# Numerators one slot behind their logits, a reordered start and a bunched end in a lookup convolution kernel

## The chip, the cores and the metric

One core of a Trainium2 chip runs the whole program. The metric is the device time of one execution in microseconds (us). Each kernel was executed several times, and medians are quoted.

## The reference, cut to what matters

Sixteen images of 256 channels and 28x28 pixels are normalised by groups of eight channels, and go through two "lookup" convolutions and a gate. Each convolution treats every channel by itself: the nine pixels of a 3x3 patch are compared with 16 learned codes, a softmax over the codes gives weights, and the weighted codes are multiplied by a matrix.

```python
def amm_conv3x3(x, centroids, w_sub, stride=1):
    ...                                            # p: patches (B, pixels, C, 9)
    d = jnp.sum(p * p, axis=-1)[..., None] - 2.0 * jnp.einsum('bncs,cks->bnck', p, centroids) \
        + jnp.sum(centroids * centroids, axis=-1)[None, None]
    attn = jax.nn.softmax(-d, axis=-1)
    lut = jnp.einsum('cks,cso->cko', centroids, w_sub)
    out = jnp.einsum('bnck,cko->bno', attn, lut)
    ...
# per image: v = gn(x); y = relu(bn1(conv1(v))); y = bn2(conv2(y))
#            y = y * sigmoid(relu(mean(y) @ w1 + b1) @ w2 + b2); out = x + relu(y + v)
```

## The kernel before

The work is laid out in slots. One slot handles 16 rows of channel pairs for half of an image's pixels: "logits" (TensorE), exponentials (ScalarE), "numerators" (TensorE, which also gives the sum of the exponentials), transposes and a reciprocal (VectorE), scaling (GpSimd), one more transpose, and some slots later the "looks", the large matmuls that accumulate the output. Sixteen slots make a stage, which is one layer of one image. There are 32 stages, and the layers of successive images alternate.

```python
ring = [p_ring.tile([P, 2, 512], F32, name=f"pair{i}") for i in range(3)]   # three pairs of PSUM banks
# pair() hands them out in turn; the two accumulators take the other two banks

epool = ctx.enter_context(tc.tile_pool(name="epool", bufs=2))               # exponentials
xpool = ctx.enter_context(tc.tile_pool(name="xpool", bufs=2))               # images
hpool = ctx.enter_context(tc.tile_pool(name="hpool", bufs=1))               # y, one buffer

def b_logits(u):          # 2 pairs x 16 matmuls 32x32
    u["lg"] = logits(u, MROW + NCH if u["maxed"] else ONE + 1)
def b_exp(u):             # one exponential for each pair
    for ps in u.pop("lg"):
        e = epool.tile([P, 2, 400], F32, tag="e", name="e")
        nc.scalar.activation(e[:, :, :n], ps[:, :, :n], AF.Exp, scale=2.0)
        u["e"].append(e)
def b_num(u):             # 2 pairs x 16 matmuls 32x32
    u["nm"] = [pair(), pair()]
    ...
```

The schedule is a table of jobs by slot and by position within the slot. On each engine the jobs are issued in that order.

```python
LC = 3                                             # looks start three slots behind
LOGITS, LOAD, MOVE, EXP, LOOK_A, NUM, TURN, SMALL, LOOK_B, MAX, LOOK_C, TURN_BACK, REST = range(13)

# stage(): one slot s
at(s, LOGITS, b_logits, u)
at(s, EXP, b_exp, u)
at(s, NUM, b_num, u)
at(s, TURN, b_turn, u)                             # VectorE: transposes of the numerators, reciprocal
at(s, TURN, c_scale, u)
at(s + 1, TURN_BACK, c_turn, u)

def norm(self, b, t):                              # statistics of image b, from slot t on
    self.at(t, REST, gn_stats, b, 0)               # VectorE, first half of the channels
    self.at(t + 1, REST, gn_stats, b, 1)           # VectorE, second half
    self.at(t + 2, SMALL, gn_mean, b)              # TensorE, then ScalarE and GpSimd
    self.at(t + 3, SMALL, gn_var, b)               # TensorE: waits for GpSimd's gn_dv
    self.at(t + 4, REST, gn_apply, b, 0)           # ScalarE writes the normalised image
    self.at(t + 5, REST, gn_apply, b, 1)

n0 = -3 if b == 1 else t - 2 * NS - 3              # the image is loaded two slots ahead
plan.at(n0 - 2, REST, load_x, b, x[b])
plan.norm(b, n0)
plan.prep(0, pat_of(0, b), {1: 1, 2: 32, 3: 56}.get(b, t - 2 * NS + 3))   # patches, written to DRAM
...
for i in range(9 * C // PART):                     # layer-2 weights: load, sort by channel, store
    plan.at(3 + i, REST, load_part, wsub2, i)
    plan.at(4 + i, REST, sort_ws2, i)
moves = ...                                        # 74 transfers that place layer 2's tables
for i, (f, *a) in enumerate(moves):
    plan.at(6 + i // 3, REST, f, *a)               # three in a slot, on the sync queue
```

Patches make a trip: GpSimd writes them to DRAM (`pat`), and the sync queue loads them for each slot (`pt`).

Of the kernel before, what the change touches and what calls it, by code (L numbers as in the profile page):

```python
# [15 lines left out]
P = 128  # L16
# [7 lines left out]
NQ = NT // 4  # L24
NLT = NQ * 9 // 4
# [44 lines left out]
def kernel(  # L70
# [82 lines left out]
    pts = [const.tile([P, 4, 400], F32, name=f"pt{i}") for i in range(6)]  # L153
    for t in pts:
        nc.sync.dma_start(t[ONE::32], view(consts, 0, [[0, 4], [0, 4], [1, 400]]))


# [6 lines left out]
    nhalf_sb = load(nhalf, "nhalf_sb")  # L164
    mones_sb = const.tile([P, 2, 32], F32, name="mones_sb")
    nc.sync.dma_start(mones_sb, mones.rearrange("l p m -> p l m"))
# [10 lines left out]
    perm = sort_sb[:, n_in : n_in + NB * C].rearrange("p (b c) -> p b c", b=NB)  # L177
    wd = [load(wd1, "wd0"), const.tile([P, NT, 32], F32, name="wd1")]
    cw = [load(cw1, "cw0"), load(cw2, "cw1")]
# [62 lines left out]
    def sort_channels():  # L242
# [19 lines left out]
        row = tpool.tile([P, 832], F32, tag="z", name="row")[:, :C]  # L262
        nc.vector.tensor_copy(row, ps[:, :C])
        own = small.tile([P, NB], F32, name="key_own")
# [29 lines left out]
    PART = 384  # L294

# [7 lines left out]
    def sort_ws1(i):  # L303

        t = parts.pop(i)
        for j in range(PART // P):
            ps = bank()
            for b in range(NB):
                nc.tensor.matmul(  # L309
                    ps[:, :C], lhsT=t[:, b, j * P : (j + 1) * P], rhs=perm[:, b], start=(b == 0), stop=(b == NB - 1)  # L310
                )
            w = ws[0][:, i * PART // P + j]
            if j == 1:
                nc.vector.tensor_copy(w, ps[:, :C])
            else:
                nc.scalar.copy(w, ps[:, :C])
# [11 lines left out]
    def sort_c2():  # L328
# [3 lines left out]
        for i in range(2):  # L332
# [7 lines left out]
            nc.scalar.dma_start(view(d_c2[i], 0, [[K * 9, P], [P * K * 9, NB], [1, K * 9]]), t)  # L340

    def sort_ws2(i):
        t = parts.pop(i)
        ps = pair()
        by_position(ps, t, PART)
        r = tpool.tile([P, 832], F32, tag="z", name="part")[:, : NB * PART].rearrange("p (b m) -> p b m", b=NB)
        nc.scalar.copy(r, ps[:, :, :PART])
        nc.scalar.dma_start(view(d_ws2, i * PART, [[9 * C, P], [P * 9 * C, NB], [1, PART]]), r)
# [53 lines left out]
    epool = ctx.enter_context(tc.tile_pool(name="epool", bufs=2))  # L402
# [59 lines left out]
    STEPS = [(dx, k, h) for dx in (1, 0, 2) for k in range(NB) for h in range(2)]  # L462

    def to_pat(l, i, pat, px=0, n=HW):
# [3 lines left out]
        nc.gpsimd.dma_start(  # L468
# [62 lines left out]
    def residual(b, k, i):  # L531
        y = ys[b][0][half(k, i)]
        nc.gpsimd.tensor_add(y, y, xs[b][half(k, i)])

# [188 lines left out]
    LC = 3  # L723
# [4 lines left out]
    class Plan:  # L728
        def __init__(self, step, lead, lb):
# [4 lines left out]
            self.end = self.ns + LC * step  # L734
# [7 lines left out]
        def emit(self):  # L742
# [7 lines left out]
            for n0, of in self.tiles:  # L750

                slots = [n0 + (LC + q) * self.step for q in range(NQ)]
# [11 lines left out]
        def stage(self, l, b, pat, s0, maxed):  # L764
            at = self.at
            for pi, px in enumerate(PXT):
                n0 = s0 + pi * NQ * self.step
                of = []
                for m in range(NQ):
# [17 lines left out]
                    at(s, NUM, b_num, u)  # L787
                    at(s, TURN, b_turn, u)
                    at(s, TURN, c_scale, u)
                    at(s + 1, TURN_BACK, c_turn, u)  # L790
                self.tiles.append((n0, of))

        def prep(self, l, pat, t):

            for i, dx in enumerate((0, 2)):
                for k in range(NB):
                    self.at(t + 4 * i + 2 + k, REST, shift, l, dx, k)
            for i in range(len(STEPS)):
                self.at(t + i, REST, to_pat, l, i, pat)

        def prep_near(self, l, pat, t, slots, t2, slots2):
# [4 lines left out]
            for i in range(len(STEPS)):  # L806
                self.at(t + i * slots // len(STEPS), REST, to_pat, l, i, pat, *PXT[0])
                self.at(t2 + i * slots2 // len(STEPS), REST, to_pat, l, i, pat, *PXT[1])

# [8 lines left out]
        def close(self, b, ob, te, pace):  # L818
# [3 lines left out]
            for n, (k, i) in enumerate((k, i) for k in range(NB) for i in range(2)):  # L822
                self.at(te + 2 + n // 2, REST, gate, b, k, i)
                self.at(te + 3 + n // pace, REST, finish, b, k, i)
                self.at(te + 4 + n // pace, REST, relu, b, k, i)
                self.at(te + 5 + n // pace, REST, residual, b, k, i)
# [11 lines left out]

    for k in range(NB):
        gn_stats(0, k)  # L840
    gn_mean(0)
    gn_var(0)
    for k in range(NB):
        gn_apply(0, k)
    for i, (dx, k, h) in enumerate(STEPS):
        if dx != 1 and h == 0:
            shift(0, dx, k)
        to_pat(0, i, d_pat[0], *PXT[0])
    square_codes(0)
    setup_codes(0)  # L850
    bn_setup()
    sort_channels()
# [3 lines left out]
    for si, (l, b) in enumerate(stages):  # L856
        t = si * NS
        plan.stage(l, b, pat_of(l, b), t, () if l == 0 else MAXED)
        if l == 0 and b >= 1:
            n0 = -3 if b == 1 else t - 2 * NS - 3  # L860
            plan.at(n0 - 2, REST, load_x, b, x[b])
            plan.norm(b, n0)
            plan.prep(0, pat_of(0, b), {1: 1, 2: 32, 3: 56}.get(b, t - 2 * NS + 3))
        if l == 1:
            if b in (0, B - 1):
                t0 = t - NS + LC
                plan.prep_near(1, pat_of(1, b), t0, 4, t0 + 4, 8)
            else:
                plan.prep(1, pat_of(1, b), 44 if b == 1 else t - 2 * NS + LC + 1)
            plan.at(t + NS, REST, load_x, b, x[b])  # L870
            plan.close(b, out[b], t + NS + LC, 1 if b < B - 2 else 2)
    for i in range(len(STEPS)):
        plan.at(i // 3, REST, to_pat, 0, i, d_pat[0], *PXT[1])
    n1 = NLT * P // PART
    for i in range(n1):
        if i < 2:
            plan.at(-6, REST, load_part, ws1, i)
            plan.at(-1, REST, sort_ws1, i)
        else:
            plan.at((i - 2) * 3 // 4 - 1, REST, load_part, ws1, i)  # L880
            plan.at((i - 2) * 3 // 4, (LOOK_A, LOOK_B)[i % 2], sort_ws1, i)
# [115 lines left out]
```

## Time and profile before

| | before |
|---|---|
| median of 3 runs | 2970.67 us (2970.14 to 2972.58) |
| span of the profiled run, granted clock | 2969.2 us, 0.989 |
| first logits start | 57.0 us |
| slots 0 to 16, 16 to 32 | 117.0 us, 103.6 us |
| a later stage, either layer | 88.3 us |
| sum of the 512 numerator groups, each from its start to the next matmul | 555.4 us |

Slot times are taken from the starts of the numerator groups in the trace.

These are groups of instructions by line. After the first bar stand their busy time in us and the mean of one in ns, after the second the engine's idle time just before them and what ended most of it. Kernel before:

```profile
L631 PE MATMUL pair<-e,cw 32*32 32x384 f32 (+1 forms) x16384 | 580.3, 502 | 11.9 <-ACT e L621 10.6
L563 PE MATMUL pair<-pt,wd 19*32 19x384 f32 (+2 forms) x18432 | 561.0, 500 | 5.9 <-DMA pt<-pat 3.3
```

There are 16384 numerator matmuls and 18432 logit matmuls over the same numbers of columns, and the fewer ones have more busy time. That is the wait hidden within "busy". The idle columns show almost nothing.

The table of waits gives total us, times and the longest. Kernel before:

```profile
DVE gn_st L417 <- DMA xt<-in_x: 23.0, 14, 2.5
...
PE pair L434 <- POOL gn_dv L428: 4.2, 14, 0.8
...
PE pair L563 <- DMA pt<-pat: 3.3, 7, 0.7
...
PE pair L563 <- DVE nt L643: 1.6, 5, 0.5
```

VectorE waits 14 times (once for each of 14 images) for an image that has not landed, 23 us in all.

### The profile page before, as it was taken

Reading aid. Unit: us, or ns where it says so; the run is one execution under the profiler, and the core shown is the slowest. Engines: PE = TensorE matmul, PEld = TensorE weight load, DVE = VectorE, ACT = ScalarE, POOL = GpSimd, SP = SyncE. Lnnn points to the kernel's source line nnn. Section 1 sums busy time; section 2 is a strip of 40 time slices with the busy share of each in tenths; the row PEclk is TensorE's granted clock in tenths of the full one; section 3 lists DMA queues with packets and bytes.
Section 4 is the critical chain, followed back from the end, with each engine's and each line's share of the span. In section 5 each row is a group of like instructions: output and inputs, shape, how many; then the busy total and the mean of one; then the engine's idle time right before and its main releaser. Section 6 shows DMA issues by size and latency. Waiting matters only on the chain. The table of waits gives total us, times and the longest.

```text
span 2969.2 us, 94838 instructions
## 1 busy us (share of the span) xinstructions
PE 2871.6 (97%) x39834; PEld 1145.4 (39%) x39834; DVE 2252.7 (76%) x2760; ACT 1092.7 (37%) x1605; POOL 1768.5 (60%) x2583
## 2 busy tenths in 40 slices
PE   4999999999999999999999999999999999999995
PEld 2433333333333333333333333333333333334332
DVE  3476777787877878787787877878788787878884
ACT  1332343433434343343433434343343434333332
POOL 3474575666656566665656656566665656656553
PEclk8999999999999999999999999999999999999998
DMA  6877777767767676776767667676776767674641
GB/s 185 227 174 170 203 219 195 212 154 213 186 169 197 151 208 174 197 185 154 211 156 207 180 180 188 154 214 156 214 185 163 200 155 206 177 189 106 163 114 56
DMA packets 296773, 530.30 MB, mean 179 GB/s; under 512 B 94240, under 2 KB 251664, under 8 KB 296336
## 3 DMA queue, kind: packets, MB, share of 16 engines
q0 software_dynamic: 51648, 269.78, 34.9%
q1 hardware_dynamic: 242512, 251.70, 32.7%
q8 instruction: 316, 5.18, 0.7%
q10 hardware_dynamic: 2176, 2.65, 0.3%
q14 instruction: 121, 0.99, 0.1%
HBM read 269.96 MB, written 254.05 MB: 176 GB/s over the span
## 4 chain that ended last, share of the span: by engine, by line
PE 79%; DMA 7%; DVE 6%; POOL 4%; issue 2%; ACT 2%; SPq 0%; ACTq 0%; DVEq 0%; POOLq 0%
PE acc L695 47%; PE pair L631 16%; PE pair L563 14%; DMA xt<-in_x 4%; DVE nt L643 2%; POOL k L659 2%; DVE rc L649 1%; DVE gn_st L417 1%; POOL total L671 1%; DMA pt<-pat 1%; ACT e L621 1%; DMA ws<-dws 1%; PE pair L309 0%; PE pair L324 0%; DVE q L677 0%
## 5 line engine op out<-in xcount | busy, mean ns | idle before, releaser
L695 PE MATMUL acc<-q,ws 128*128 128x384 f32 (+1 forms) x4096 | 1641.0, 519 | 9.7 <-ACT y L717 9.7
L659 POOL TENSOR_TENSOR k<-nt,rc 128x832 f32<-128x832 f32 (+1 forms) x512 | 802.3, 1567 | 1132.9 <-DVE rc L649 1120.5
L643 DVE STREAM_TRANSPOSE nt<-pair 128x832 f32<-128x832 f32 (+1 forms) x1024 | 976.3, 992 | 603.5 <-PE pair L631 506.4
L621 ACT ACTIVATE e<-pair 128x800 f32<-128x800 f32 (+1 forms) x1024 | 787.8, 821 | 1358.8 <-PE pair L563 1357.3
L695 PEld LDWEIGHTS acc<-q,ws 128*128 128x128 f32 x4096 | 696.9, 189 | 907.7 <-issue 577.2
L631 PE MATMUL pair<-e,cw 32*32 32x384 f32 (+1 forms) x16384 | 580.3, 502 | 11.9 <-ACT e L621 10.6
L563 PE MATMUL pair<-pt,wd 19*32 19x384 f32 (+2 forms) x18432 | 561.0, 500 | 5.9 <-DMA pt<-pat 3.3
L677 DVE STREAM_TRANSPOSE q<-k 128x832 f32<-128x832 f32 (+1 forms) x512 | 489.1, 955 | 0.8 <-POOL k L659 0.8
L649 DVE RECIPROCAL rc<-nt 128x104 f32<-128x104 f32 (+1 forms) x512 | 398.5, 778 | 17.6
L631 PEld LDWEIGHTS pair<-e,cw 32*32 32x32 f32 x16384 | 167.5, 103 | 349.2 <-ACT e L621 321.4
L563 PEld LDWEIGHTS pair<-pt,wd 19*32 19x32 f32 (+1 forms) x18432 | 138.4, 103 | 340.1 <-issue 265.5
L665 POOL TENSOR_TENSOR tail<-nt,rc 128x104 f32<-128x104 f32 (+1 forms) x512 | 242.4, 473 | 0.0
L695 PE MATMUL acc<-qt,ws 128*128 128x400 f32 (+1 forms) x512 | 218.6, 509 | 0.0
L671 POOL TENSOR_TENSOR total<-total,nt 128x96 f32<-128x96 f32 (+1 forms) x448 | 198.7, 443 | 0.0
L468 POOL DMA_DIRECT2D pat<-side x280 | 186.6, 667 | 1.1 <-DMA pat<-im 0.7
L671 POOL TENSOR_TENSOR total<-total,rc 128x96 f32<-128x96 f32 (+1 forms) x448 | 175.5, 392 | 0.0
L695 PEld LDWEIGHTS acc<-qt,ws 128*128 128x128 f32 x512 | 90.8, 189 | 100.1 <-issue 50.6
L587 DVE TENSOR_REDUCE mx<-z 128x48 f32<-128x768 f32 (+1 forms) x128 | 120.8, 943 | 0.0
L582 DVE STREAM_TRANSPOSE z<-pair 128x768 f32<-128x768 f32 (+1 forms) x128 | 119.2, 969 | 0.0
L468 POOL DMA_DIRECT2D pat<-im x140 | 94.0, 672 | 3.5 <-ACT im L447 3.5
L707 ACT ACTIVATE im<-acc,bnsh,bnsc 128x384 f32<-128x384 f32 (+1 forms) x64 | 43.4, 678 | 139.4 <-PE acc L695 133.4
L717 ACT ACTIVATE y<-acc,bnsh,bnsc 128x384 f32<-128x384 f32 (+1 forms) x64 | 43.4, 679 | 91.7 <-PE acc L695 76.8
(106 smaller groups left out, 753.5 us busy)
## 6 DMA issues: line engine op xcount, KB each, us to landing
pat<-side POOLq DMA_DIRECT2D x232, 588.0 KB, 6.1
pt<-pat SPq DMA_DIRECT2D x1024, 112.5 KB
pt<-pat SPq DMA_DIRECT2D x1024, 108.0 KB
pat<-im POOLq DMA_DIRECT2D x116, 588.0 KB, 5.3
xt<-in_x POOLq DMA_DIRECT2D x32, 784.0 KB, 8.8
out_dram<-y POOLq DMA_DIRECT2D x16, 784.0 KB, 4.0
pat<-side POOLq DMA_DIRECT2D x24, 300.0 KB, 6.1
pat<-side POOLq DMA_DIRECT2D x24, 288.0 KB, 6.0
```

The costliest lines, as they stand in the source:

```text
L468: nc.gpsimd.dma_start(view(pat, (ROWS * p0 + 9 * k + 3 * dx) * HW + px, [[ROWS * HW, m], [HW, 3], [1, n]]), bass.AP(v.tensor, v.offset, [l ...
L563: nc.tensor.matmul(ps[t // 2][c : c + 32, t % 2, :n], lhsT=wd[l][32 * i : 32 * i + rows, 4 * u["m"] + t, :], rhs=u["pt"][32 * i : 32 * i + ...
L587: nc.vector.tensor_reduce(u["mx"][:, 2 * v : 2 * v + 2].rearrange("p t (j b) -> p t b j", j=2)[:, :, :nb], u["z"].pop(0)[:, : 64 * nb].rea ...
L621: nc.scalar.activation(e[:, :, :n], ps[:, :, :n], AF.Exp, scale=2.0)
L631: nc.tensor.matmul(u["nm"][t // 2][32 * i : 32 * i + 32, t % 2, :n], lhsT=cw[l][c : c + 32, 4 * u["m"] + t, :], rhs=es[t // 2][c : c + 32, ...
L643: nc.vector.transpose(nt[:, :nb, 2 * v : 2 * v + 2].rearrange("p b t r -> p t b r"), ps[:, :, : 32 * nb].rearrange("p t (b r) -> p t b r", ...
L649: nc.vector.reciprocal(rc[:, : 8 * nb], u["nt"][:, :, SUM])
L659: nc.gpsimd.tensor_tensor(q[:, :nb].rearrange("p b (a s) -> p (b a) s", s=8), nt[:, :, :8], rc.unsqueeze(2).to_broadcast([P, 8 * nb, 8]), ...
L665: nc.gpsimd.tensor_tensor(tails[key][:, :nb, 8 * (m % 4) : 8 * (m % 4) + 8], nt[:, :, 8].rearrange("p (b a) -> p b a", a=8), rc.rearrange( ...
L671: nc.gpsimd.tensor_add(t[:, : 8 * nb], t[:, : 8 * nb], v)
L677: nc.vector.transpose(q[:, :, : 32 * nb].rearrange("p h (b r) -> p h b r", r=32), u.pop("k")[:, :nb].rearrange("p b (h r) -> p h b r", h=2),)
L695: nc.tensor.matmul(accs[key][:, :n], lhsT=ws[l][:, 2 * m + h if h < 2 else 2 * NQ + m // 4, o * P : (o + 1) * P], rhs=u["q"][h][:, :n], st ...
```

## The change

Three things were rebuilt. First, the numerators of a slot run in the next slot, so that their exponentials are done when TensorE comes to them. Four exponential buffers take the place of two, and looks start four slots behind. Second, the start is reordered: channels are sorted while the image loads, patches of the first image are written by halves of the channels and partly through the sync queue, the first weights are loaded at once into three patch buffers that are still unused, and image 1 is prepared later. Some of this reaches beyond the start: the new order of patch writes holds for all images, and the layer-2 weights are copied by VectorE and stored through GpSimd, no longer by ScalarE. Third, the last two images' closing steps are bunched, with half of the final relu and addition fused on VectorE. The core of the diff, with cuts marked:

```diff
-    epool = ctx.enter_context(tc.tile_pool(name="epool", bufs=2))
+    epool = ctx.enter_context(tc.tile_pool(name="epool", bufs=4))
...
-    LC = 3
+    LC = 4
...
-                    at(s, NUM, b_num, u)
-                    at(s, TURN, b_turn, u)
-                    at(s, TURN, c_scale, u)
-                    at(s + 1, TURN_BACK, c_turn, u)
+                    at(s + 1, NUM, b_num, u)
+                    at(s + 1, TURN, b_turn, u)
+                    at(s + 1, TURN, c_scale, u)
+                    at(s + 2, TURN_BACK, c_turn, u)
...
-    STEPS = [(dx, k, h) for dx in (1, 0, 2) for k in range(NB) for h in range(2)]
+    STEPS = [(dx, k, h) for h in range(2) for dx in (1, 0, 2) for k in range(NB)]
...
+    bn_setup()
+    row = sort_keys()
+    square_codes(0)
     for k in range(NB):
         gn_stats(0, k)
     gn_mean(0)
     gn_var(0)
+    sort_ranks(row)
+    setup_codes(0)
     for k in range(NB):
         gn_apply(0, k)
-    for i, (dx, k, h) in enumerate(STEPS):
-        if dx != 1 and h == 0:
+    for i, (dx, k, h) in enumerate(STEPS[: len(STEPS) // 2]):
+        if dx != 1:
             shift(0, dx, k)
-        to_pat(0, i, d_pat[0], *PXT[0])
-    square_codes(0)
-    setup_codes(0)
-    bn_setup()
-    sort_channels()
+        to_pat(0, i, d_pat[0], *PXT[0], eng=nc.gpsimd if dx == 0 else nc.sync)
...
-            n0 = -3 if b == 1 else t - 2 * NS - 3
-            plan.at(n0 - 2, REST, load_x, b, x[b])
+            n0 = 3 if b == 1 else t - 2 * NS - 3
+            plan.at(n0 - (4 if b == 1 else 2), REST, load_x, b, x[b])
             plan.norm(b, n0)
-            plan.prep(0, pat_of(0, b), {1: 1, 2: 32, 3: 56}.get(b, t - 2 * NS + 3))
+            plan.prep(0, pat_of(0, b), {1: 9, 2: 33, 3: 57}.get(b, t - 2 * NS + 3), 0.67 if b == 1 else 1)
...
+                if pace == 4 and n % 2:
+                    self.at(te + 4, REST, relu_residual, b, k, i)
+                else:
+                    self.at(te + 4 + n // pace, REST, relu, b, k, i)
+                    self.at(te + (4 if pace == 4 else 5 + n // pace), REST, residual, b, k, i)
...
-            plan.close(b, out[b], t + NS + LC, 1 if b < B - 2 else 2)
+            plan.close(b, out[b], t + NS + LC, 1 if b < B - 2 else 4)
```

## The prediction

> **What bounds the kernel now.** I read the page first, then the table of waits, then one slot of the timeline, then the chain of waits at both ends. A slot is the work on one group of 16 channel rows: logits on TensorE, exponentials on ScalarE, numerators on TensorE, transposes and reciprocals on VectorE, scaling on GpSimd, and some slots later the "looks" (the big accumulating matmuls). There are 32 stages (16 images, two layers) of 16 slots.
>
> The engine shares:
> ```profile
> PE 2871.6 (97%) x39834; PEld 1145.4 (39%) x39834; DVE 2252.7 (76%) x2760; ACT 1092.7 (37%) x1605; POOL 1768.5 (60%) x2583
> ```
> TensorE is the bound, and VectorE, the next, has a quarter to spare. But 97% busy isn't 97% at full rate. One slot, in order of time:
> ```profile
> 1207.84 0.95 PE L563 MATMUL pair<-pt,wd 21*32 21x400 f32 x32
> ...
> 1208.72 1.56 PE L695 MATMUL acc<-q,ws 128*128 128x384 f32 x4
> 1208.91 1.57 ACT L621 ACTIVATE e<-pair 128x800 f32<-128x800 f32 x2 [2.70 <-PE pair L563]
> ...
> 1210.21 0.50 PEld L631 LDWEIGHTS pair<-e,cw 32*32 32x32 f32 x32 [0.55 <-ACT e L621]
> 1210.21 1.22 PE L631 MATMUL pair<-e,cw 32*32 32x400 f32 x32
> ```
> L563 (logits) and L631 (numerators) are the same 32 small matmuls. Logits start at 1208.72 - 1207.84 = 0.88 us before what follows. Numerators start at 1210.21 and the next look at 1211.36 (same view): 1.15. The second exponential ends at 1210.48, in the middle of the numerators, so their second half waits for it. Over the whole trace I took, from each numerator group's start to that of the next matmul, 512 groups: 555.4 us, median 1.07, best tenth 0.88. At 0.88 each they would be 450.6. So **some 105 us are waits inside numerator groups**, hidden in "busy". The table of waits shows the same pair, larger, because weight loads run ahead and wait while looks still stream:
> ```profile
> PEld pair L631 <- ACT e L621: 321.4, 555, 7.1
> ...
> PE pair L631 <- ACT e L621: 10.6, 20, 6.4
> ...
> PE acc L695 <- ACT y L717: 9.7, 1, 9.7
> ```
> Last, the ends. The first logits start at 57.01 us:
> ```profile
> 48.73 8.34 PE L309 MATMUL pair<-sort_sb,part 128*128 128x256 f32 x24 [0.25 <-ACT gn_gm L425]
> ...
> 57.01 0.93 PE L563 MATMUL pair<-pt,wd 19*32 19x384 f32 x32
> ```
> and near the end the chain is, in order of time:
> ```profile
> 2900.03 1.96 POOL y L533 x2
> 2901.99 0.29 issue
> 2902.28 8.21 DMA out_dram<-y
> ```
> The buffer y exists once. Image 15's first half can't be evacuated until image 14's store has landed at 2910.5; TensorE waits 9.7 us there.
>
> **What the Trainium skill says.** "TensorE: Matmul & The Clock Gate", section "Part 3: Packing small matmuls — row/col tiling": matmuls start and end strictly in program order, while weight loads may be pulled ahead. The trace agrees: a numerator group blocks the looks behind it, and loads show 321 us of waiting where matmuls show 10.6. "PSUM — Partial Sum Buffer", "Specifications (TRN2)": eight banks. The kernel uses six for its ring of three pairs and two for accumulators, so a later numerator can't be given a fourth pair; the order of reuse decides (below). "DMA: Bandwidth & Descriptors", "Issuing engines are not separate DMA queues": all queues run on the same 16 engines and a second issuer saves issue time only. So moving patch writes from GpSimd to the sync queue buys no bandwidth; in the windows, DMA is 80% busy with 208 GB/s from 57 to 178 us. The clock gate's cold state, in the first page's section "What's actually happening", fits the granted clock of 0.68 from 25 to 50 us; it returns to 1.00 by 100 us.
>
> **The change part by part.**
>
> *Numerators one slot behind.* No instruction is added. Numerators of slot s-1 run in slot s, with four exponential buffers in place of two; looks start four slots behind, not three, so the distance from scaling to looks is kept. What can still hold a group is the ring: per slot the pairs go logits a, logits b, numerators a, numerators b, and with three pairs numerators b reuse the pair of this slot's logits a, which the first exponential must have read. In the trace the first exponential ends a median 0.52 us before the numerators start (best nine tenths: at least 0.46), the second 0.15 before the second half. So the new wait is nearly always met already. Of 105 us I credit **100**, less 5 for the gap between image load and its statistics: VectorE waits there for the image (14 times, up to 2.5 us, logits then up to 2.2 us late), and slots 0.2 us shorter leave that load less time. **Net 95.**
>
> *The start.* Before, TensorE's order was statistics of image 0 (12.3), code squares (27.2, behind GpSimd's issue of 12 patch writes), sort keys and ranks (VectorE, 33.5 to 43.1), sorting of two weight parts (8.3 us), first logits at 57. After, with durations from this trace: vecs land near 5 instead of 9.7 (first on the queue); normalisation constants and keys to 12; statistics of image 0, 2.4 us, to 14.3; ranks, 5.9 us, to 20; code adds, 2.8 us, to 23; sort of the constants to 25; three weight parts at 4.17 us each to 37.7. On the other side statistics lead to the normalised image at 21, shifts at 24, half of the patches (1.8 MB). By then 7.0 MB have been asked for (image 0.8, tables 4.4, patches 1.8), at 200 to 220 GB/s some 33 us, plus the first 0.43 MB patch load: about 37. The two meet: **first logits near 39, 18 earlier**, with one weight part fewer left (2.9 us). Also gone: the 7.1 us that ScalarE spent at 69 to 76 us waiting to overwrite image 0 while its patches were still being written, which kept numerators 6.4 us; image 1 is now normalised six slots later. Together 28. Against it: in slots 0 to 3 there are no looks to fill TensorE, and image 1's 7 MB of patches fall into slots 9 to 16, beside loads and table moves, some 10 MB in 40 us, above the 245 GB/s that the best window shows. I take 6 off: **22**.
>
> *The end.* For images 14 and 15 the closing steps run at four per slot, with half of the relu and residual fused on VectorE. Store of image 14: issue falls a slot (5.2 us) plus 2 us of residual adds earlier relative to the evacuation. Numerators of the slot at T, store at T+6.3 (transposes 2.0, reciprocal 0.8, scaling 1.6, tail 0.45, waits), landed at T+14.5, needed at T+14.5: of 9.7 some **8.5** go. After the last look: four GpSimd adds run 2953.68 to 2957.60; with two of four on VectorE they end near 2955.4: **2.2**. The fourth look slot at the end adds nothing: TensorE streams 10.9 us of looks there without a gap, and has the same looks to do.
>
> *Untouched:* the slow passage at 227 to 281 us, where layer 2's tables are placed through the sync queue (stage 103.6 us in place of 88). Its waits are for transfers, so numerators save little there; 3 off.
>
> Sum: 95 + 22 + 10.7 - 3 = 125, giving 2846. A check from below: looks 1746 (2304 matmuls of 0.372 and as many of 0.386), numerators 451, logits 502 (576 groups at 0.872), small ones 21 make 2720; first logits 39, sorting and table matmuls after it 28, late logits 26, numerator waits 5, weak first slots 5, after the last look 19: 2842. I say **2843**.
>
> **Rivals.** *The wait moves.* The ring's rule makes numerators b wait for ScalarE anyhow, or VectorE becomes the bound in layer 2 stages. For: those stages show VectorE 74.0 us busy of 88, and four transposes and reductions more in slots that take maxima. Against: TensorE needs about 86.7 there, and VectorE holds a two-slot lead before looks. If a third of the gain went so: 2875. *The start is DMA bound.* For: 0.80 busy from 57 to 178 us and 20 us less room for the same bytes. Then start gains 8, not 22: 2857. *Waits were free.* If the recorded group length were an artefact, the middle gains nothing: 2938. Against: the second half's start follows the end of the second exponential by 0.1 us, and a stage takes 88.3 us where looks, logits and numerators at full rate make 82.4 and 85.9.
>
> **Range and chances.** Better start and no lost overlap: 2822. Both first rivals: 2890. Range 2815 to 2885. Faster by over 2% means under 2912; only the third rival or a new stall in every stage prevents it. Chances 0.95, 0.04, 0.01.
>
> **What would show it.** Numerator groups at a median near 0.88 us; stages near 83.5 and 87, mean 85.3; first logits at 36 to 43; image 1's first numerators near 145 instead of 177.8; the wait for y under 3 us; VectorE near 79%. The prediction fails if numerators wait as before for the exponential, if logits wait for VectorE's transposes in most slots, if patch loads stop TensorE before slot 20, or if the granted clock falls below 0.98.

## The result, and the profile after

| | before | after |
|---|---|---|
| median of 3 runs | 2970.67 us | 2896.00 us (2894.12 to 2904.20) |
| ratio of the times | | 0.9754, 95% interval 0.9724 to 0.9784 |
| span of the profiled run, granted clock | 2969.2, 0.989 | 2894.4, 0.988 |
| first logits start | 57.0 | 37.4 |
| slots 0 to 16, 16 to 32 | 117.0, 103.6 | 116.0, 109.5 |
| later stages, layer 1 and layer 2 | 88.3, 88.3 | 84.0, 87.1 to 90.7 (the last of them 84.4) |
| sum of numerator groups, median of one | 555.4, 1.07 | 466.8, 0.88 |

A ratio is the mean time of one kernel's runs over that of the other's of the same rounds, so it is not quite the ratio of the medians quoted.

The kernel is 74.7 us faster. The prediction said 127.7, with a range that ended at 2885. So 53 us of the gain are missing.

One stage in the table is a control that the kernel brings with it. Of the 13 layer-2 stages in the middle, only the last has no next image whose statistics fall into it. It took 84.4 us, the others 87.1 to 90.7. It is spared that image's load too, so this is a hint and not yet a test.

First, the engine shares and the two groups of small matmuls on the page of the kernel after:

```profile
PE 2797.8 (97%) x39834; PEld 1105.5 (38%) x39834; DVE 2258.5 (78%) x2770; ACT 1090.3 (38%) x1595; POOL 1766.8 (61%) x2577
...
L578 PE MATMUL pair<-pt,wd 19*32 19x384 f32 (+2 forms) x18432 | 575.6, 501 | 33.7 <-DVE nt L658 18.1
...
L646 PE MATMUL pair<-e,cw 32*32 32x384 f32 (+1 forms) x16384 | 485.1, 501 | 0.3 <-DVE nt L658 0.2
```

Numerators fell from 580.3 to 485.1 us of busy time, and their idle time is gone. Logits rose from 561.0 to 575.6 and their idle time from 5.9 to 33.7. One ordinary slot of the kernel after, in order of time, shows why numerators no longer wait:

```profile
1204.58 0.95 PE L578 MATMUL pair<-pt,wd 19*32 19x400 f32 x32
...
1205.65 1.57 ACT L636 ACTIVATE e<-pair 128x800 f32<-128x800 f32 x2 [3.95 <-PE pair L578]
...
1207.01 0.95 PE L646 MATMUL pair<-e,cw 32*32 32x400 f32 x32
...
1207.89 1.61 PE L710 MATMUL acc<-q,ws 128*128 128x400 f32 x4
```

Numerators start at 1207.01 while this slot's exponentials still run (to 1207.22). They use those of the slot before. The next look starts 0.88 us later, where it took 1.15 before. But in the same image's next slot, logits are split in two:

```profile
1208.49 1.03 DVE L428 BATCH_NORM_STATS2 gn_st<-xt 128x6 f32<-128x392 f32 x2 [1.05 <-DMA xt<-in_x]
...
1209.43 0.90 PE L578 MATMUL pair<-pt,wd 19*32 19x400 f32 x16
...
1209.69 1.94 DVE L658 STREAM_TRANSPOSE nt<-pair 128x832 f32<-128x832 f32 x2
...
1210.75 0.91 PE L578 MATMUL pair<-pt,wd 19*32 19x400 f32 x16 [0.42 <-DVE nt L658]
```

VectorE reaches the statistics of the next image, waits 1.05 us for its load, and spends 1.03 us on them. Only then does it transpose the numerators that ended near 1207.9. The second half of the logits needs the PSUM pair which that transpose frees, and starts 1.32 us after the first half instead of some 0.44. The brackets show 0.42 us of it. The Trainium skill, "PSUM — Partial Sum Buffer", section "Engine vs sequencer instructions", says that the queues of ScalarE, VectorE and GpSimd are strictly first in, first out. The trace agrees: two transposes started 2.7 us after their numerators (1207.01 to 1209.69), where those of the slot before had started 1.1 us after theirs (1202.15 to 1203.23), because an instruction that waited for a transfer stood ahead of them.

The table of waits of the kernel after has this as its first line on TensorE:

```profile
DVE gn_st L428 <- DMA xt<-in_x: 25.5, 14, 2.7
...
PE pair L578 <- DVE nt L658: 18.1, 15, 2.0
PE pair L445 <- POOL gn_dv L439: 17.4, 14, 1.3
...
PE pair L578 <- DMA pt<-pat: 9.3, 6, 3.8
...
PE pair L335 <- DMA part<-in_wsub: 8.5, 1, 8.5
```

VectorE's own wait hardly changed (23.0 to 25.5). TensorE's wait for VectorE rose from 1.6 to 18.1, and its wait for GpSimd's input to the variance matmul (L445, L434 before) from 4.2 to 17.4. That second wait grew mostly because TensorE comes earlier. At 12 of the 14 images GpSimd's square is done some 5.8 us after the start of the matmul for the mean before the change, and 6.2 after it. The numerators just ahead of the variance matmul start 5.15 us after that matmul before, and 4.49 after. In three of the middle stages, a third cost follows. This is TensorE after a late half of logits, and then the windows over it (the busy times of PE, PEld, DVE, ACT and POOL with their counts, the granted clock, the DMA share and GB/s):

```profile
1556.39 0.91 PE L578 MATMUL pair<-pt,wd 19*32 19x400 f32 x16 [1.94 <-DVE nt L658]
1557.23 1.70 PE L710 MATMUL acc<-q,ws 128*128 128x400 f32 x2
```

```profile
1552.00:1556.00 4.00, 2.45 (x32) 0.86 (x20) 1.83 (x4) 0.84 (x1) 0.93 (x2) 1.00 0.85 270
...
1558.00:1560.00 2.00, 2.00 (x4) 1.01 (x3) 1.97 (x5) 0.36 (x1) 1.80 (x2) 0.50 0.61 216
```

The clock falls from 1.00 to 0.50, and six looks take 3.90 us in place of 2.21. In the three stages together this costs 4.5 us (3.90, 3.90 and 3.35 against 2.21).

At the start, first logits come when the prediction had them, but a wait for the layer-2 weights follows. TensorE's timeline of the kernel after, and the same 25 us in the windows of both kernels (after, then before; the last two columns are the share of time that the DMA engines are busy and the GB/s):

```profile
37.42 3.96 PE L578 MATMUL pair<-pt,wd 19*32 19x384 f32 x32 [3.52 <-DMA pt<-pat]
...
74.75 5.07 PE L335 MATMUL pair<-part,sort_sb 128*128 128x384 f32 x8 [8.51 <-DMA part<-in_wsub]
```

```profile
50.00:75.00 25.00, 16.09 (x253) 7.01 (x222) 15.42 (x22) 6.22 (x11) 13.74 (x21) 0.88 0.85 232
```

```profile
50.00:75.00 25.00, 21.30 (x220) 13.73 (x219) 8.02 (x12) 6.69 (x15) 8.06 (x15) 0.91 0.64 154
```

In this stretch TensorE is busy for 16.09 of 25 us after, and 21.30 before. DMA is busier, at 0.85 against 0.64. The start now runs into its transfers.

At the end, from TensorE's and VectorE's timelines of the kernel after:

```profile
2814.87 2.69 DVE L536 SCALAR_TENSOR_TENSOR y<-xt,gn_rstd,y 128x392 f32<-128x392 f32 x4
...
2837.91 3.04 PE L710 MATMUL acc<-q,ws 128*128 128x400 f32 x4 [2.28 <-ACT y L732]
```

The wait for the single y buffer fell from 9.7 to 2.28 us. But VectorE now does four closing steps in one piece, and the second half of the logits behind it starts 1.0 us late: the two halves take 2.8 us (2816.59 to 2819.42), against 1.6 with the old closing steps (a run below).

The trace can be cut at numerator groups into three parts. After the change a slot's numerators come one slot, 5.2 us, after its logits, so 5.2 us are added to what their starts show. "Predicted" splits the prediction's own terms; its 95 us for the numerators is shared out over 32 stages.

| part | before | after | gain | predicted gain |
|---|---|---|---|---|
| up to slot 48 | 368.8 | 363.5 less 5.2 | 10.5 | 22 - 3 + 95 x 3/32 = 27.9 |
| the next 26 stages | 2297.3 | 2241.5 | 55.8 | 95 x 26/32 = 77.2 |
| the rest | 303.1 | 289.4 plus 5.2 | 8.5 | 10.7 + 95 x 3/32 = 19.6 |
| sum | | | 74.8 | 124.7 |

So the loss is in three places: 17 us in the first 48 slots, 21 in the middle and 11 at the end.

### The profile page after: what moved, and what is told of

It reads as the page before. It is cut to its first block, busy times and chain, and to the rows that moved or that the text cites.

```text
span 2894.4 us, 94782 instructions
## 1 busy us (share of the span) xinstructions
PE 2797.8 (97%) x39834; PEld 1105.5 (38%) x39834; DVE 2258.5 (78%) x2770; ACT 1090.3 (38%) x1595; POOL 1766.8 (61%) x2577
## 4 chain that ended last, share of the span: by engine, by line
PE 77%; DMA 9%; POOL 6%; issue 4%; DVE 3%; ACT 0%; SPq 0%; POOLq 0%; DVEq 0%; ACTq 0%
PE acc L710 49%; PE pair L578 15%; PE pair L646 13%; DMA xt<-in_x 4%; DMA pt<-pat 3%; POOL k L674 2%; POOL total L686 1%; DVE nt L658 1%; POOL pat L479 1%; POOL tail L680 1%; DVE rc L664 1%; DVE gn_st L428 1%; DMA pat<-side 1%; PE pair L335 1%; DMA part<-in_wsub 0%
## 5 line engine op out<-in xcount | busy, mean ns | idle before, releaser
L578 PE MATMUL pair<-pt,wd 19*32 19x384 f32 (+2 forms) x18432 | 575.6, 501 | 33.7 <-DVE nt L658 18.1
L646 PE MATMUL pair<-e,cw 32*32 32x384 f32 (+1 forms) x16384 | 485.1, 501 | 0.3 <-DVE nt L658 0.2
L646 PEld LDWEIGHTS pair<-e,cw 32*32 32x32 f32 x16384 | 119.9, 103 | 290.2 <-issue 146.5
L544 POOL TENSOR_TENSOR y<-y,xt 128x392 f32<-128x392 f32 x60 | 65.9, 1099 | 10.4 <-ACT y L540 10.4
```

What stands on the lines that cost most here:

```text
L578: nc.tensor.matmul(ps[t // 2][c : c + 32, t % 2, :n], lhsT=wd[l][32 * i : 32 * i + rows, 4 * u["m"] + t, :], rhs=u["pt"][32 * i : 32 * i + ...
L646: nc.tensor.matmul(u["nm"][t // 2][32 * i : 32 * i + 32, t % 2, :n], lhsT=cw[l][c : c + 32, 4 * u["m"] + t, :], rhs=es[t // 2][c : c + 32, ...
```

## The experiments

All 14 kernels were timed in three rounds against the kernel before on the same chip. Two of the kernels give wrong results, and are marked. All others were correct. A part of one profiled run is less certain than a median. Slots 0 to 16 took 116.0 to 119.7 us, and slots 16 to 32 took 105.4 to 109.5, in the kernel after and in the run with the old closing steps, which changes nothing there.

### The parts alone, and their sum

**Numerators alone**, on the kernel before:

```diff
-epool bufs=2, LC = 3
+epool bufs=4, LC = 4
-                    at(s, NUM, b_num, u)            # and the three jobs after it
+                    at(s + 1, NUM, b_num, u)        # and the three jobs after it, one slot later
-                plan.prep_near(1, pat_of(1, b), t0, 4, t0 + 4, 8)
+                plan.prep_near(1, pat_of(1, b), t0, 3, t0 + 4, 8)   # or loads come before their patches
```

> The kernel before with only the numerators one slot behind (four exponential buffers, looks four slots behind). Theory 1 (the wait for the second exponential goes nearly whole, but the gap between image load and statistics and the gn_var wait give back some 2.5 us an image): numerator groups at 0.88 us, time 55 to 65 us under the kernel before, near 2910. Rival (the whole of the 105 us in numerator groups comes back, and the shortfall of the changed kernel lies at its ends alone): 85 to 95 us under, near 2880.

Measured: 2904.36 us, ratio 0.9774 (0.9750 to 0.9798), a gain of 68, a little over the first theory's 55 to 65 and well under the rival's 85. Its 26 middle stages took 2241.6 us, those of the full change 2241.5: in the middle this part is all of the change. Layer-1 stages took 84.0 us, layer-2 stages 87.2 to 92.7. TensorE waited 14.4 us for VectorE's transposes and 17.3 for the variance input, as in the full change. So these two waits come with the numerators' shift, not with the new start. The wait for y fell to 5.1 us by this part alone, because the fourth look slot gives the store more time.

**The start alone**, on the kernel before (the new order of the first stages, patches by halves of the channels, image 1 later):

```diff
+all of the change but LC, epool bufs, the numerators' slot and the closing steps
```

> The changed kernel with numerators in their own slot again (two exponential buffers, looks three slots behind) and the old closing steps: the new start alone. Theory 1 (the first slots and the placing of layer 2's tables are bound by transfers, so the 19 us by which the first logits come earlier are largely lost again): 8 to 14 us under the kernel before. Rival (the start keeps what it wins, and the loss comes from the numerators colliding with it): 20 us or more under.

Measured: 2953.05 us, ratio 0.9937 (0.9913 to 0.9961), a gain of 19.5, between the two expectations (8 to 14, and 20 or more). The trace splits it: 12.4 us at slot 48 and 9.3 over the 26 middle stages (2288.0 us against 2297.3). The second part is not a start at all: the numerator groups took 543.3 us in place of 555.4. I put that down to the new order of patches, which moves ScalarE's shifted copies away from the exponentials, but have not tried it alone.

**The end alone**, on the kernel before:

```diff
-            plan.close(b, out[b], t + NS + LC, 1 if b < B - 2 else 2)
+            plan.close(b, out[b], t + NS + LC, 1 if b < B - 2 else 4)   # with relu_residual, as in the change
```

> The kernel before with only the closing steps of the last two images at four a slot. Theory 1: the wait for y shrinks from 9.7 us, but the closing steps on VectorE, bunched in two slots, hold up transposes for 2 to 3 us: 4 to 8 us under the kernel before. Rival (the step is free on VectorE): 10 us or more under.

Measured: 2958.19 us, ratio 0.9960 (0.9932 to 0.9989), a gain of 14 by the medians and 12 by the ratio: the rival's 10 or more, not the theory's 4 to 8. The wait of 9.7 us for y is gone from the table.

**The change with the old closing steps** (the edit above, reversed, on the kernel after):

```diff
-            plan.close(b, out[b], t + NS + LC, 1 if b < B - 2 else 4)
+            plan.close(b, out[b], t + NS + LC, 1 if b < B - 2 else 2)   # without relu_residual
```

> The changed kernel with the closing steps of the last two images as they were before (two a slot). Theory 1 (the fourth slot between numerators and looks had already taken half of the wait for y, and the bunched closing on VectorE costs 3 us of logits): 0 to 5 us over the changed kernel, wait for y near 5.8 us. Rival (the new closing is worth what it was alone, 12 us): 10 us or more over.

Measured: 2898.60 us, ratio 0.9753 (0.9734 to 0.9772), against 0.9754 for the full change. The closing steps are worth 12 us alone, and beside the numerators' shift nothing that these times can tell from zero. The traces tell more. What follows the middle stages took 292.1 us in this run and 291.9 with the numerators alone, but 285.4 to 289.4 in the ten kernels that have the shift and the new closing steps (289.4 in the kernel after), so 2 to 7 us remain. The wait for y was 5.4 us in this run, so they save 3.1 us of it, and the logits that they delay take part of that back.

What follows: alone, the parts make 68 + 19.5 + 12, some 100 us, and together 75. About 9 us of the overlap is the numerator wait that start and numerators both remove, and about 4.5 us of the wait for y (9.7 to 5.1 or 5.4) is removed by the fourth look slot as well as by the closing steps. The other 10 or so are not accounted for one by one; the start's lead that is lost in its transfers, below, is the likely part.

### The waits in the middle

Two theories were set against each other. In the first, the image's load is too late, and each late image holds VectorE and then TensorE. In the second, VectorE has become the bound, or the pair of layer-2 stages costs more for another reason.

**Load two slots earlier**, on the kernel after:

```diff
-            plan.at(n0 - (4 if b == 1 else 2), REST, load_x, b, x[b])
+            plan.at(n0 - 4, REST, load_x, b, x[b])
```

> The changed kernel with each image's load for the statistics issued two slots earlier. Theory 1 (VectorE stands at the statistics until the image lands, and the logits' second pair waits behind the transposes it holds up, 2.1 to 3.8 us for each of 14 images): those waits go, logits' lateness falls under 1 us an image, time 25 to 35 us under the changed kernel, near 2866. Rival (VectorE is simply too full in these slots, whatever the load does): within 5 us of the changed kernel.

Measured: 2892.49 us (2882.83 to 2899.88), ratio 0.9733 (0.9697 to 0.9769). That is 3.5 us, not what the theory wanted. But its waits say more than its time:

```profile
PE pair L445 <- POOL gn_dv L439: 17.7, 14, 1.3
PE pair L578 <- DMA pt<-dm: 16.1, 5, 4.2
PE pair L578 <- DMA pt<-pat: 12.8, 6, 5.9
...
PE pair L578 <- DVE nt L658: 1.5, 2, 1.0
```

The wait for VectorE went from 18.1 to 1.5 us, so the late image was its cause. In its place came 16.1 us for the maxima's trip through DRAM (4.1 in the kernel after) and more for patches: the load now meets those transfers. The middle also had five stretches at half clock where the kernel after had three. The experiment moved a transfer and so could not settle what the wait is worth.

**Statistics two slots later**, with the load where it was:

```diff
-            plan.norm(b, n0)
+            plan.norm(b, n0 + (0 if b == 1 else 2))
```

> The changed kernel with the statistics of each image taken two slots later, the load left where it is. After the run with the earlier load, in which the logits' wait behind the statistics went (layer 2 stages 86.3 us in place of 88.3) but 7 of 14 image pairs got a new wait of 3 to 4 us for the maxima's trip through DRAM, which the earlier load ran into. Theory 1 (what is missing is distance between load and statistics, and the collision came of moving the load): both waits gone, nearly every layer 2 stage at 86.3, time 25 to 35 us under the changed kernel, near 2865. Rival (TensorE needs the transfer share either way; waits only move): within 8 us of the run with the earlier load.

Measured: 2872.33 us (2871.03 to 2877.31), ratio 0.9665 (0.9648 to 0.9682), 23.7 us under the kernel after, just short of the 25 to 35 expected and far from the rival, which allowed 8 us from the run before. VectorE no longer waits for an image, TensorE waits 1.5 us for VectorE, and no transfer wait grew in its place (5.4 us for the maxima). The variance matmul, which follows the statistics, now falls into layer-1 stages. These took 86.5 us, and layer-2 stages mostly 84.4.

**The variance matmul one slot later too:**

```diff
-            self.at(t + 3, SMALL, gn_var, b)
-            self.at(t + 4, REST, gn_apply, b, 0)
-            self.at(t + 5, REST, gn_apply, b, 1)
+            self.at(t + 4, SMALL, gn_var, b)
+            self.at(t + 5, REST, gn_apply, b, 0)
+            self.at(t + 6, REST, gn_apply, b, 1)
-            plan.prep(..., t - 2 * NS + 3), ...)
+            plan.prep(..., t - 2 * NS + 4), ...)
```

> As the run before, and the variance matmul and what hangs on it one slot later still. Theory 1: the 1.35 us by which a numerator group and the variance matmul after it wait for GpSimd's square of the deviation, once for each of 14 images, go: 15 to 19 us under the run with the statistics alone, near 2848, all of the middle at the rate that the prediction had. Rival (that wait only takes the place of a later one): no difference over 5 us.

Measured: 2855.79 us (2853.25 to 2858.15), ratio 0.9602 (0.9585 to 0.9619), 40 us under the kernel after. The waits on TensorE:

```profile
PE pair L578 <- DMA pt<-pat: 13.9, 10, 6.8
...
PE pair L578 <- DVE nt L658: 1.5, 2, 1.0
...
PE pair L445 <- POOL gn_dv L439: 1.1, 1, 1.1
```

The waits for patches are those of the first 48 slots. VectorE, at the same place of the run as shown above:

```profile
1204.76 0.99 DVE L428 BATCH_NORM_STATS2 gn_st<-xt 128x6 f32<-128x392 f32 x2
...
1205.93 1.98 DVE L658 STREAM_TRANSPOSE nt<-pair 128x832 f32<-128x832 f32 x2
```

The statistics start without a bracket: nothing is waited for. Layer-2 stages took 84.4 us and layer-1 stages 85.4, almost without exception. The 26 middle stages took 2208.4 us, 88.9 less than before the change, where the prediction's terms give 77.2. The half-clock stretches of the middle are gone too, and 4.5 us of the 40 are theirs. VectorE as the bound is ruled out: it does the same work in this kernel, and a pair of stages takes 169.8 us where the prediction wanted 170.5.

**The variance alone:**

```diff
 the edit above, with the statistics left at slot n0
```

> The changed kernel with only the variance matmul and what follows it one slot later; the statistics stay. Statistics two slots later alone made 2872.3 and both 2855.8, so the variance was worth 16.5 after the statistics. Theory (two separate waits that add up): 2879, within 2876 to 2884, with TensorE's wait for GpSimd's variance input near zero and the logits' wait for VectorE unchanged at 1.5 to 2 us an image. Rival (one delay seen at two places: VectorE, held by the image, is late with the statistics and so with the variance): within 5 us of 2896.

Measured: 2881.63 us (2877.34 to 2889.00), ratio 0.9688 (0.9669 to 0.9707), 14.4 under the kernel after. The expectation was 2876 to 2884.

```profile
PE pair L578 <- DVE nt L658: 17.2, 15, 2.5
...
PE pair L445 <- POOL gn_dv L439: 1.1, 1, 1.1
```

One wait went and the other stayed. 23.7 and 14.4 make 38.1, and both edits together gained 40.2: two separate waits that add up.

**The same edit on the kernel before:**

```diff
 statistics two slots later, variance, normalisation and patch writes one slot later still; on the kernel before
 (image 1: its patch writes go from slot 1 to slot 2 as well)
```

> The kernel before, with the statistics of each image two slots later and its variance matmul and normalisation another slot later, nothing else. Theory (the image wait grew with the change because the numerators no longer hid it: before, logits were late by 0.4 to 1.3 us an image and the variance wait was 4.2 us in all): 10 to 25 us under the kernel before, 2946 to 2961. Rival (these waits were there in full before the change and the change only failed to touch them): 35 to 45 us under it, about 2931, as much as the same edit gained on the changed kernel (40).

Measured: 2955.61 us (2955.00 to 2959.60), ratio 0.9941 (0.9923 to 0.9958), a gain of 17 where the changed kernel gained 40. Its waits for the image and for VectorE's transposes are gone, and one remains of the other:

```profile
PE pair L434 <- POOL gn_dv L428: 0.8, 1, 0.8
```

But the variance matmul now stands 0.4 us behind a step of the gate on ScalarE, 13 times, 5.6 us in all (`PE pair L434 <- ACT se_hid L489` in the table of waits). So the old kernel did pay for late images and the late variance input: 17 us, or some 23 if that new wait is added back, and not the 5.8 (1.6 + 4.2) that its table of waits shows. The change made the price 40. The difference, 17 to 23 us, accounts for most or all of the middle's loss of 21. The traces of the 26 middle stages agree: the edit shortened them by 33.1 us on the changed kernel and by 12.4 here, 20.7 less.

The run also bears on the worth of the numerators' shift where no image is late: 2284.9 us for the 26 middle stages of this kernel against 2208.4 with the change, 76.5 us, or 94 for 32 stages. Some 11 of the 76.5 are two small waits that only this kernel has there (the 5.6 us above, and 5.3 of the mean's matmul for VectorE's statistics), so 81 to 94. The prediction had put 100 on it.

### The first 48 slots

**Table moves in another order.** In the kernel after, patch loads stand in the sync queue among the moves of layer 2's tables up to 264 us. The theory was that the long moves, which come last and together, hold the sync queue:

```diff
+    first, mid, late = moves[:18], moves[18:50], moves[50:]
+    moves = first + [late.pop(0) if i % 7 in (2, 4, 6) and late else mid.pop(0) for i in range(56)]
```

> The changed kernel with the 24 long table moves of layer 2's weights spread over slots 12 to 30 between the short ones, in place of a block in slots 22 to 30. Theory 1 (the passage at 200 to 275 us is bound by the moves' own transfers on the sync queue, which is why the start's gain is lost there): patch waits in the passage fall from some 26 us to under 10, time 8 to 16 us under the changed kernel. Rival (the passage is bound by the bytes of patches, moves or not): within 4 us.

Measured: 2897.93 us, ratio 0.9746 (0.9730 to 0.9763): no gain, as the rival said. Slots 16 to 32 were 6 us shorter in the profiled run. The run with the old closing steps has them 4 us shorter with nothing changed there, so this shows little.

**Layer-2 weights sorted one slot later**, on the best kernel so far, and **with the interleaved moves as well**:

```diff
-        plan.at(4 + i, REST, sort_ws2, i)
+        plan.at(5 + i, REST, sort_ws2, i)
```

> Statistics and variance later, as in the best kernel so far (2855.8 us), and the sort of the layer-2 weights placed one slot after its place there, with the loads where they were. In the changed kernel TensorE stood 8.5 us at 64.7 us for the first of these loads. Theory (the wait is a matter of order): the stall goes, 2847 us, within 2845 to 2850. Rival (the start is bound by bytes, DMA busy 0.85 at 232 GB/s there, so that another transfer is waited for instead): within 4 us of 2855.8.

> The previous kernel with the long table moves of layer 2 interleaved with the short ones. Theory (the passage at 180 to 270 us is bound by what must be moved; interleaving gave nothing in the changed kernel, 2897.9 against 2896.0): within 5 us of the previous run. Rival (the gain of 6 us that the stage from slot 16 to 32 showed was lost in image waits that are now gone): 5 to 12 us under it.

Measured: 2851.08 us (2848.27 to 2856.99), ratio 0.9596 (0.9576 to 0.9616), and 2851.13 us (2847.82 to 2858.36), ratio 0.9598 (0.9577 to 0.9619). The first fell between its two expectations and is inconclusive: its wait for these weights fell from 6.8 to 3.2 us in the profiled runs, and slot 48 came at 350.2 in place of 361.7 us, but its interval overlaps that of the kernel it was built on, 0.9585 to 0.9619. The second gained nothing over the first, as its theory said. These two are the fastest kernels. They are 45 us under the kernel after the change.

Two orders of the same transfers had given little. So the transfers themselves were taken away, with the engines' work kept.

**No table moves** (wrong results), on the kernel after:

```diff
-    moves += [(place_cw2, i, t, j) for j in range(NCH) for i in range(4) for t in range(4)]
-    moves += [(place_ws2, i, t, j) for j in range(NCH) for i in range(4) for t in range(2)]
-    moves += [(place_tail, i, j) for j in range(NCH) for i in range(4)]
+    for i in range(NLT // 2):
+        plan.at(14 + i, REST, nc.gpsimd.memset, ws[1][:, 2 * i : 2 * i + 2], 0.0)
```

> The changed kernel without the 56 moves of layer-2 numerator codes and weights into their places; the weight table is filled with zeros by GpSimd in slots 14 to 22 (wrong results on purpose). TensorE, VectorE and ScalarE do the same work. In the changed kernel slots 16 to 32 took 109.5 us against 103.6 before and some 100.6 predicted. Theory (these slots are held by transfers: the moves and what queues behind them): slots 16 to 32 fall by 9 to 22 us, the time to 2874 to 2887. Rival (image patches, cold clock or engine work hold them): within 4 us of 2896.

Measured: 2879.03 us (2876.47 to 2882.29), ratio 0.9685 (0.9666 to 0.9705), 17 us under the kernel after. Slots 16 to 32 took 89.6 us, in place of 109.5 in the kernel after and 105.4 in the run with the old closing steps.

**No layer-2 weight traffic either** (wrong results; TensorE sorts resident data with the same matmuls):

```diff
-        t = parts.pop(i)
+        t = ws[0][:, 0:3].rearrange("p t c -> p (t c)").rearrange("p (b m) -> p b m", b=NB)
-        nc.gpsimd.dma_start(view(d_ws2, i * PART, ...), r)
-        plan.at(3 + i, REST, load_part, wsub2, i)
```

> The previous kernel, and the layer-2 weights are not loaded or stored at all: TensorE sorts resident data in their place (same matmuls and copies, wrong results on purpose), 4.7 MB less moved in slots 3 to 10. In the changed kernel slots 0 to 16 took 116.0 us against 117.0 before and some 105 predicted, with one wait of 8.5 us for the first of these loads. Theory (bytes hold the first slots): slots 0 to 16 fall by 9 to 14 us beside what the previous run gained, the time to 2862 to 2876. Rival (the order of engine work holds them and another wait takes the place of the 8.5 us): within 4 us of the previous run.

Measured: 2865.44 us (2860.55 to 2870.26), ratio 0.9633 (0.9614 to 0.9652), another 13.6. Slots 0 to 16 took 107.5 us, 8.5 less than in the kernel after and 11.7 less than in the run before this one. In the window that was shown for the start:

```profile
50.00:75.00 25.00, 24.60 (x340) 11.52 (x339) 17.77 (x26) 8.03 (x14) 13.76 (x21) 1.00 0.84 237
```

TensorE is busy for 24.60 of 25 us where it was 16.09. DMA is as busy as before, at 0.84: other transfers take the room, and nothing on TensorE waits for them. Both theories were met, so these transfers hold this kernel for 31 us by the medians (28 in the traces of the first 32 slots: 109.5 - 89.6 and 116.0 - 107.5). Whether it is their bytes, their small packets or their places in the queues, these two runs do not separate. It remains open how much of this the transfers cost in the kernel before. That was not tried.

## Why the prediction was wrong, point by point

- **Numerators one slot behind, 100 us before deductions: right in its mechanism, a little high.** The median group is 0.88 us as foretold, the sum fell by 88.6, and with the late images out of the way the shift is worth 81 to 94. The ring of PSUM pairs made no new wait. The rival in which VectorE becomes the bound in layer 2's stages did not come: those stages took 84.4 us with the images' waits removed, under the 87 that the prediction wanted.
- **"less 5 for the gap between image load and its statistics": this term failed first.** The mechanism had been seen, its size had not: removal was worth 40 us after the change and 17 to 23 before, so the change cost 17 to 23 there in place of 5. Three things were missed. The 14 loads that statistics wait for take as long as ever (median 10.0 us before, 10.1 after) while two slots of the kernel are shorter. The second half of the logits waits for a transpose, so it inherits VectorE's wait and the statistics' own 1 us as well. And the variance matmul's wait for GpSimd, 0.3 us for most images before, was 1.2 us for each image, mostly because TensorE came to it earlier; it was not in the prediction at all.
- **Readings that hid this.** "Logits then up to 2.2 us late" is the length of the longest such group in the middle; it was 1.3 us late. The prediction put the logits of the maxima into layer 2 alone (stages of 83.5 and 87). In the trace every middle stage runs 18 groups of logits, and without waits the two kinds take 84.0 us (kernel after) and 84.4 (its one stage without statistics, and the runs with later statistics). So a layer-2 stage of 88 us looks near the forecast and holds 4 us of waits. And the check from below, 2842, allowed 26 us for late logits, where the logit groups of the kernel after took 556.6 us, 54 above its 502. That the two sums agreed confirmed nothing.
- **The start, 22 us: the time of the first logits was right, the rest was not.** First logits came at 37.4 us, within the stated 36 to 43. At slot 48, with the numerators' share, 27.9 us were expected and 10.5 measured. Image 1's first numerators came at 165.7 us, not near 145. The failed step is "I take 6 off" for transfers, together with "3 off" for the passage of table moves. The second rival, that the start is bound by its transfers and gains 8, was nearly what happened. The last two experiments show that transfers hold the new start: the same kernel without them is 31 us faster. That the missing 17 us went there is likely, but as their cost in the kernel before was not measured, it is not shown.
- **The end, 10.7 us: mis-sized by overlap.** The wait for y fell to 2.3 us as foretold, but the fourth look slot took half of it by itself (5.1 us with numerators alone), and the four closing steps in a row on VectorE held up one slot's logits by about 1.2 us. Beside the numerators' shift the closing steps are worth nothing that the run times show, and 2 to 7 us in the traces.
- **The checks listed last.** VectorE is at 78% (79 foretold), the granted clock at 0.988 (above 0.98). The mean middle stage took 86.2 us (85.3 foretold). Patch loads did not stop TensorE between the first logits and slot 20, but the layer-2 weights did, for 8.5 us. Logits waiting for transposes were named as a way to fail "in most slots". It came in one or two slots of each image, and that was enough.
- **The range was cut short.** The prediction itself put 2890 on "both first rivals" and ended the range at 2885. Both losses came: a transfer-bound start, and a new wait in the middle, the latter for a reason other than the one given.

## What to carry to other kernels

When a wait is removed from every slot, look at each rarer wait that sits beside it, and give it the size it has when nothing hides it. A few us in the table of waits may stand for several times as much: 5.8 us were worth 17 or more in the kernel before, though 35.5 (18.1 + 17.4) were worth 40 in the kernel after. One engine's wait is passed to what stands behind it in its queue. Moving the consumer (statistics two slots later) cost nothing that the runs show and worked, while moving the transfer made it collide with another. And when two new orders of a start's transfers have given no clear gain, as here, taking the transfers away for one wrong run tells at once what they are worth.

## What the Trainium skill lacked or had wrong

- "TensorE: Matmul & The Clock Gate", section "What's actually happening", has the clock cold, at half, after an idle window of about 3.4 us. Half is right (0.50 granted), but in the middle of the kernel after, single gaps of 1.94, 1.55 and 1.09 us were enough: six looks took 3.9 us, and 3.35 in one case, in place of 2.21. It happened at 3 of 14 images. A gap of 2.04 us in the same trace was not followed by it, and the runs do not show what decides. (Another section of that page, "A second HAM failure mode: psum-queue depth-cycling", lets short pauses do it, but gives no length.)
- "PSUM — Partial Sum Buffer", section "Engine vs sequencer instructions", states strict order for VectorE's queue, and the traces agree. What it lacks is the consequence for PSUM: 25.5 us of VectorE waiting for images cost 23.7 us of run time (by the run with later statistics) through the pairs that VectorE had not yet freed. In the kernel before, 23.0 us of the same wait cost, together with the variance wait, no more than the 17 to 23 us found above.
- "DMA: Bandwidth & Descriptors", section "Measured (HBM→SBUF, 128 partitions, SWDGE, issued from GpSimd)", gives 6.15 us for 1 MB, as the time of the transfer alone, without its issue. Here the 14 image loads of 784 KB that statistics wait for took 8.8 to 10.8 us from issue to landing (median 10.1), with the DMA engines about three quarters busy with this and other queues. The section has no figure for a transfer beside the same core's other queues, and that is the one a schedule needs.
